# Source gathers in four groups of two, attributes' loads from ScalarE's queue, target rows loaded one pair earlier, in an edge-attention kernel

## Chip, cores and metric

The kernel runs on one core of a Trainium2 chip. The metric is the device time of one execution in microseconds (us). Three executions of the kernel before took 5886.15, 5887.58 and 5853.44 us; the median, 5886.15 us, is the time before.

## What is computed

One layer of graph attention over 12,500 nodes with 128 channels and 400,000 edges, the edges sorted by target. Cut to what matters:

```python
msg_src = h @ w_src + b_src                  # h: layer-normed, rectified nodes
msg_dst = h @ w_dst
message = msg_src[edge_src] + msg_dst[edge_dst]
rad_w   = mlp(edge_attr_32)                  # 32 -> 64 -> 64 -> 128, SiLU
message = message * edge_weight * rad_w
message = message @ w_sep + b_sep            # 8 heads: 16 alpha, 16 value channels each
score   = sum(leaky(alpha) * alpha_dot)      # per edge and head
att     = segment_softmax(score, edge_dst)
out     = segment_sum(value * att, edge_dst) @ w_proj + b_proj
```

The result is added to the node input. All arithmetic is float32, apart from a split of the target rows into three bfloat16 parts.

## The kernel before, in words

The nodes' products come first and are written to two tables in device memory, `t_src` and `t_dst`. The main part, `windows()`, goes over the edges in 400 pairs of two sections. A section has 500 edges in four tiles of 125, so a pair has eight tiles. The sections' edges are sorted by target, so a section touches a window of 64 target rows.

The order of work is written out by hand in `step(k)` (L955). Each engine executes its own instructions in that order; semaphores set by the framework make one engine wait for another. One call of `step(k)` holds work of several pairs, so that they overlap:

- Loads on SyncE's queue (SP), three to six pairs ahead: edge weights (`load_w`, L716), target rows (`load_md`, L720, with two addresses read from `base`, L722), targets (`load_d`, L709, on odd k, for two pairs), edge attributes (`load_e`, L705: 125 x 8 x 32 numbers in runs of 128 bytes), stores of window sums (L926, L929), scores (L841) and maxima (L875).
- Gathers of source rows on GpSimd (POOL): `gather(k, f)` (L739) issues four indirect DMAs (L744), one for each tile of section f, into a tile `gs0` or `gs1` with four buffers. It stands behind `sources(k, f)` (L803), which reads the buffer that the gather refills for the pair four later.
- TensorE (PE), in this order in a step: third layer of the attributes' network of pair k (`mlp3`, L795); transposes of section 1's gathered rows (`sources`, L808) into the PSUM tile `pm1`; `message` (L816), which adds the target rows by a one-hot product; values of the first section of pair c = k - 12 (L908); alpha product of section 0 (`alphas`, L825); first layer of pair k + 2 (L763); values of the second section of c (L908); transposes of section 0 of pair k + 1 (L808, `pm0`); alpha product of section 1 (L825); second layer of pair k + 1 (L778); window sums of c (`sums`, L919); transposes of the attributes of pair k + 3 (`e_T`, L754); on odd k the scores of two pairs (`scores`, L836).
- VectorE (DVE): `rad` (L799) from the third layer and the edge weights, `mT` (L821) from `pm0`, `pm1` and `rad`, `al` (L829) and `pvx` (L910) among others.
- ScalarE (ACT): the SiLUs `sl` (L827), `h1` (L766) and `h2` (L781), the copies `ob` (L923) and `eT` (L756), casts of target rows (`split_md`, L730 and L735) and others. In the loop it issues no DMA.

Most PSUM tiles have one buffer; `V`, `pa`, `misc`, `p3`, `pm0` and `pm1` are each reused in every step. After the last pair the values of the last twelve pairs use `pm0` and `pm1` (L905). The softmax over eight pairs and the combination of windows at the end are not touched by the change.

## Time and profile before

| what | value |
|---|---|
| median of three executions | 5886.15 us |
| profiled execution: time, span | 5892.37 us, 5890.6 us |
| mean granted TensorE clock | 0.892 of full speed |
| busy: TensorE, VectorE, ScalarE, GpSimd | 78%, 53%, 32%, 53% of the span |
| gathers (L744) | 3,200, 970 ns each |
| moved by DMA | 794.76 MB, mean 135 GB/s |
| issues of attributes' loads on SP (L707) | 400 |
| PE waiting for gathered rows (L808) | 1.6 us, once |

The span is the stretch from the first to the last instruction of the profiled execution. Busy times are unions of the instructions of an engine; a busy TensorE is not one at its peak, since the ends of its products are modelled. In rows of waits the columns are: engine and line that waited, what released it, us in total, times, longest. "issue" there means that the profile shows nothing that was waited for, "remote" that the releaser isn't known. In a timeline the columns are: start, length, engine, line, operation, and in brackets the idle time of the engine before it with what ended it. The granted clock of TensorE is 1.00 or 0.50 at any moment; a mean is given for a stretch.

### The profile page before, as it was taken

The page shows a single profiled execution, that of the slowest core. Times are in us where ns is not written, and L with a number is a line of the kernel's source. Part 1 is how long each engine was busy: PE and PEld are TensorE (multiplying, and loading weights), DVE is VectorE, ACT ScalarE, POOL GpSimd, SP SyncE. Part 2 cuts the span into 40 slices and gives each one's busy share as a digit, 9 for nine tenths or more (in the row PEclk, how much of TensorE's full clock was granted, in tenths as well). Part 3 has the DMA queues.
Part 4 walks back from the last instruction along what each step waited for, and adds up shares of the span by engine and source line. Part 5 has one row for each costly group of instructions (what it writes and reads, how often), then busy time and mean ns, then how long its engine had stood idle before and what let it go on. Part 6 is the DMA issues. An engine that isn't in the chain of part 4 may idle for free.

```text
span 5890.6 us, 88077 instructions
## 1 busy us (share of the span) xinstructions
PE 4616.9 (78%) x29692; PEld 2541.0 (43%) x29692; DVE 3100.6 (53%) x6005; ACT 1909.7 (32%) x4595; POOL 3119.2 (53%) x3223
## 2 busy tenths in 40 slices
PE   5688788787877788777877887787887887787874
PEld 3244444444444444444444444444444444444444
DVE  5345555555555555555555554555555555455566
ACT  4233333333333333333333333333333333333331
POOL 1655555555555555555555555555555555555520
PEclk8788988898989999899898998999998989888897
DMA  5565555555555555555565555555555555555533
GB/s 194 156 142 133 136 129 135 139 138 128 143 129 139 144 131 135 132 138 132 137 139 132 140 132 129 128 132 131 137 130 135 127 132 136 127 132 127 132 89 143
DMA packets 901338, 794.76 MB, mean 135 GB/s; under 512 B 530271, under 2 KB 776975, under 8 KB 900747
## 3 DMA queue, kind: packets, MB, share of 16 engines
q1 hardware_dynamic: 796664, 572.15, 36.4%
q0 software_dynamic: 102816, 210.37, 17.9%
q10 hardware_dynamic: 1394, 6.53, 0.3%
q8 instruction: 234, 3.83, 0.3%
q14 instruction: 230, 1.88, 0.1%
HBM read 648.39 MB, written 140.67 MB: 134 GB/s over the span
## 4 chain that ended last, share of the span: by engine, by line
PE 70%; another core or an unknown queue 9%; DVE 8%; issue 7%; ACT 4%; DMA 1%; SPq 1%; POOL 0%; ACTq 0%; POOLq 0%; DVEq 0%
PE V L908 14%; PE pa L825 13%; PE pm L808 8%; PE p L795 8%; PE misc L919 7%; PE pm L816 5%; PE misc L836 4%; PE p L763 4%; PE p L778 4%; PE m L754 3%; DVE mT L821 2%; DVE rad L799 2%; DVE pvx L910 1%; ACT sl L827 1%
## 5 line engine op out<-in xcount | busy, mean ns | idle before, releaser
L744 POOL DMA_INDIRECT gs<-t_src,idx x3200 | 3104.8, 970 | 2537.2 <-PE pm L808 1152.5
L827 ACT ACTIVATE sl<-pa,c_b_a 128x500 f32<-128x500 f32 x800 | 541.9, 677 | 2419.9 <-PE pa L825 1302.9
L825 PE MATMUL pa<-mT,c_w_a 128*128 128x500 f32 x1600 | 933.4, 668 | 451.4 <-DVE mT L821 276.0
L908 PE MATMUL V<-c_w_v,mT 128*125 128x128 f32 x6208 | 987.6, 307 | 198.3 <-DVE pvx L910 171.7
L799 DVE SCALAR_TENSOR_TENSOR rad<-p,c_fc_b,w_b 128x500 f32<-128x500 f32 x800 | 553.2, 733 | 1096.5 <-PE p L795 623.9
L908 PEld LDWEIGHTS V<-c_w_v,mT 128*125 128x125 f32 x6208 | 829.3, 207 | 518.7 <-issue 274.7
L829 DVE SCALAR_TENSOR_TENSOR al<-pa,sl 128x500 f32<-128x500 f32 x800 | 542.3, 678 | 654.3 <-ACT sl L827 396.0
L910 DVE TENSOR_TENSOR pvx<-V,Pem 125x512 f32<-125x512 f32 x776 | 533.2, 687 | 588.7 <-remote 180.6
L821 DVE SCALAR_TENSOR_TENSOR mT<-pm,c_b_src,rad 128x500 f32<-128x500 f32 x800 | 555.1, 733 | 207.4 <-remote 112.2
L919 PE MATMUL misc<-pvx,oh 125*64 125x136 f32 x6400 | 475.7, 292 | 123.2 <-DVE oh L898 75.1
L808 PE MATMUL pm<-ident,gs 125*128 125x125 f32 x3200 | 561.2, 303 | 1.6 <-DMA gs<-t_src,idx 1.6
L808 PEld LDWEIGHTS pm<-ident,gs 125*128 125x128 f32 x3200 | 404.3, 156 | 343.9 <-issue 341.6
L795 PE MATMUL p<-h,w3b 64*128 64x500 f32 x1600 | 495.8, 699 | 34.5 <-ACT h L781 27.1
L919 PEld LDWEIGHTS misc<-pvx,oh 125*64 125x64 f32 x6400 | 372.2, 141 | 290.1 <-issue 183.1
L825 PEld LDWEIGHTS pa<-mT,c_w_a 128*128 128x128 f32 x1600 | 267.7, 210 | 511.0 <-DVE mT L821 310.9
L836 PE MATMUL misc<-al,w_s 128*32 128x500 f32 x1600 | 243.5, 679 | 236.9 <-ACT ob L923 122.9
L816 PE MATMUL pm<-ohT,m 64*128 64x500 bf16 x2400 | 340.6, 392 | 0.0
L763 PE MATMUL p<-eT,w1b 64*128 64x250 f32 x1600 | 309.4, 467 | 1.0 <-ACT eT L756 1.0
L923 ACT COPY ob<-misc 128x136 f32<-128x136 f32 x400 | 109.0, 273 | 619.4 <-PE m L754 308.2
L781 ACT ACTIVATE h<-p,b 128x500 f32<-128x500 f32 x400 | 269.8, 674 | 97.5 <-remote 77.4
L778 PE MATMUL p<-h,w2b 64*64 64x250 f32 x3200 | 278.7, 421 | 9.2 <-ACT h L766 7.7
L766 ACT ACTIVATE h<-p,b 128x500 f32<-128x500 f32 x400 | 272.9, 682 | 27.3 <-remote 14.9
(145 smaller groups left out, 3259.2 us busy)
## 6 DMA issues: line engine op xcount, KB each, us to landing
w_b<-in_edge_weight SPq DMA_DIRECT2D x400, 500.0 KB
d_b<-in_dst SPq DMA_DIRECT2D x400, 250.0 KB
gs<-t_src,idx POOLq DMA_INDIRECT x3200
e_t<-in_edge_attr SPq DMA_DIRECT2D x400, 125.0 KB
sc_d<-Sp SPq DMA_DIRECT2D x200, 250.0 KB
win<-ob SPq DMA_DIRECT2D x400, 68.0 KB
agg<-ob SPq DMA_DIRECT2D x800, 33.5 KB
md<-t_dst SPq DMA_DIRECT2D x800, 32.0 KB
```

Source lines behind the costliest of these rows:

```text
L744: nc.gpsimd.indirect_dma_start(out=gs[:, j, :], out_offset=None, in_=t_src[:, :], in_offset=bass.IndirectOffsetOnAxis(ap=idx[:, t:t + 1], ...
L763: nc.tensor.matmul(p1[:, q, 0:2 * T], w1b[s, :], eTs[k][s, :], start=True, stop=True)
L795: nc.tensor.matmul(p3[:, f, 0:SEC], w3b[s, :], h2s[k][s, :], start=True, stop=True)
L799: nc.vector.scalar_tensor_tensor(rad[:, s], p3[:, f, 0:SEC], b3, w_g[k][:, s], op0=ALU.add, op1=ALU.mult)
L808: nc.tensor.matmul(pms[k, f][:, t * T:(t + 1) * T], gs[:T, t, :], ident[:T, :T], start=(t == 0), stop=False, is_transpose=True, skip_group ...
L816: nc.tensor.matmul(pm[f], m3[k][s, j, :], ohT[k][s, :], start=False, stop=(j == 2), skip_group_check=True)
L821: nc.vector.scalar_tensor_tensor(mTs[k][:, s], pm[f], b_n, rad[:, s], op0=ALU.add, op1=ALU.mult)
L825: nc.tensor.matmul(pa, w_a, mTs[k][:, f * SEC:(f + 1) * SEC], start=True, stop=True)
L827: nc.scalar.activation(sl, pa, AF.Silu, bias=b_a, scale=1.0)
L908: nc.tensor.matmul(V[:, t, :], mTs[c][:, o:o + T], w_v, start=True, stop=True)
L910: nc.vector.tensor_mul(pvx[c][:, f, :, 0:C].rearrange("p t (h k) -> p t h k", h=H), V.rearrange("p t (h k) -> p t h k", h=H), Pem[c // MP] ...
L919: nc.tensor.matmul(acc[f * W:(f + 1) * W, :], ohs[c][:, f * TS + t, :], pvx[c][:, f, t, :], start=(t == 0), stop=(t == TS - 1), skip_group ...
```

## The change

- A gather group is split: `gather(k, f, h)` and `sources(k, f, h)` handle two tiles each, h = 0 or 1, with tiles `gs00`, `gs01`, `gs10`, `gs11` of half the size and four buffers each. The number of gathers, transposes and bytes stays.
- The four groups have new places in `step`. For pair k + 1: section 0's first half where the whole section stood (ahead of the second alpha product), its second half behind that product, section 1's first half behind the window sums and the softmax, ahead of `e_T`. Section 1's second half stays behind `mlp3` in the pair's own step.
- `load_e` is issued on ScalarE's queue and stands behind `alphas(k, 0)`; before it was on SP's, at the beginning of the step.
- `load_md` runs four pairs ahead instead of three, with five buffers instead of four.

```diff
             def load_e(k):
                 e_g[k] = lp.tile([T, 8, RAD], F32, name="e_t", bufs=4)
-                nc.sync.dma_start(out=e_g[k], in_=ea_t[k])
+                nc.scalar.dma_start(out=e_g[k], in_=ea_t[k])
...
-                md[k] = lp.tile([P, C], F32, name="md", bufs=4)
+                md[k] = lp.tile([P, C], F32, name="md", bufs=5)
...
-            def gather(k, f):
-                gs = lp.tile([P, TS, C], F32, name=f"gs{f}", bufs=4)
+            def gather(k, f, h):
+                gs = lp.tile([P, TS // 2, C], F32, name=f"gs{f}{h}", bufs=4)
                 idx, _ = prep[k // 16]
-                for j in range(TS):
-                    t = k % 16 * 8 + f * TS + j
+                for j in range(TS // 2):
+                    t = k % 16 * 8 + f * TS + h * 2 + j
...
-            def sources(k, f):
-
-                gs = gath.pop((k, f))
-                pms[k, f] = pp.tile([C, SEC], F32, name=f"pm{f}")
-                for t in range(TS):
-                    nc.tensor.matmul(pms[k, f][:, t * T:(t + 1) * T], gs[:T, t, :], ident[:T, :T],
+            def sources(k, f, h):
+
+                gs = gath.pop((k, f, h))
+                if h == 0:
+                    pms[k, f] = pp.tile([C, SEC], F32, name=f"pm{f}")
+                for j in range(2):
+                    t = 2 * h + j
+                    nc.tensor.matmul(pms[k, f][:, t * T:(t + 1) * T], gs[:T, j, :], ident[:T, :T],
...
                 if has(k + 3):
                     load_w(k + 3)
-                    load_md(k + 3)
+                if has(k + 4):
+                    load_md(k + 4)
...
-                if has(k + 6) and k >= -4:
-                    load_e(k + 6)
...
                 rad = mlp3(k) if has(k) else None
                 if has(k):
-                    sources(k, 1)
+                    sources(k, 1, 1)
                 if has(k + 4):
-                    gather(k + 4, 1)
+                    gather(k + 4, 1, 1)
...
                     alphas(k, 0)
+                if has(k + 6) and k >= -4:
+                    load_e(k + 6)
...
                 if has(k + 1):
-                    sources(k + 1, 0)
+                    sources(k + 1, 0, 0)
                 if has(k + 5):
-                    gather(k + 5, 0)
+                    gather(k + 5, 0, 0)
                 if has(k):
                     alphas(k, 1)
+                if has(k + 1):
+                    sources(k + 1, 0, 1)
+                if has(k + 5):
+                    gather(k + 5, 0, 1)
...
                     elif r == 3:
                         softmax_T(m - 1)
+                if has(k + 1):
+                    sources(k + 1, 1, 0)
+                if has(k + 5):
+                    gather(k + 5, 1, 0)
                 if has(k + 3):
                     e_T(k + 3)
```

More of the change, by code (lines that the diff above doesn't have):

```diff
@@ L746, in gather @@
                         in_offset=bass.IndirectOffsetOnAxis(ap=idx[:, t:t + 1], axis=0))
-                gath[k, f] = gs
+                gath[k, f, h] = gs
             def e_T(k):
```

## The prediction, made before the result was known

> **What bounds the kernel now.** I read the page first (busy shares, the chain that ended last), then the waits of every engine, then the timeline and the granted clock of a few steps in the middle of the pair loop.
>
> ```profile
> PE 4616.9 (78%) x29692; PEld 2541.0 (43%) x29692; DVE 3100.6 (53%) x6005; ACT 1909.7 (32%) x4595; POOL 3119.2 (53%) x3223
> PE 70%; another core or an unknown queue 9%; DVE 8%; issue 7%; ACT 4%; DMA 1%; SPq 1%; POOL 0%; ACTq 0%; POOLq 0%; DVEq 0%
> ```
>
> TensorE (PE) makes the time, but 30% of the chain is not PE's; the DMA share of the chain is 1%, so no load or gather that arrives late holds the end. The chain in order of time gives the length of a step, from one third-layer product (L795) to the next:
>
> ```profile
> 3003.85 1.04 PE p L795 x4
> 3019.57 1.04 PE p L795 x4
> 3028.85 1.04 PE p L795 x4
> ```
>
> 15.7 us and then 9.3 us. Over pairs 20 to 380 the mean is 13.9 us; the shortest steps take 9.27 us. An odd pair has one product group more (L836, 1.05 us), but odd steps take some 17 us against 10 us for even ones. So some 4 us a pair are lost. Where, the waits of PE tell:
>
> ```profile
> PE pa L825 <- DVE mT L821: 276.0, 164, 5.1
> PE V L908 <- DVE pvx L910: 171.7, 66, 5.4
> PE pa L825 <- issue: 127.6, 57, 22.2
> PE misc L836 <- ACT ob L923: 122.9, 53, 5.7
> PE misc L836 <- issue: 88.5, 78, 2.0
> PE misc L880 <- ACT ob L923: 53.1, 37, 3.9
> ```
>
> PE waits for VectorE and ScalarE, which are busy 53% and 32%. They are late because they learn late that PE is done. The timeline shows it:
>
> ```profile
> 3082.46 0.95 POOL L744 DMA_INDIRECT gs<-t_src,idx  x1 [0.30 <-PE V L908]
> 3083.22 1.10 PE L825 MATMUL pa<-mT,c_w_a 128*128 128x500 f32 x2 [1.25 <-issue]
> 3086.22 0.94 POOL L744 DMA_INDIRECT gs<-t_src,idx  x1 [0.30 <-issue]
> 3089.22 0.69 DVE L910 TENSOR_TENSOR pvx<-V,Pem 125x512 f32<-125x512 f32 x1 [5.41 <-remote]
> 3089.31 1.28 ACT L827 ACT_TABLE_LOAD   x1 [7.11 <-remote]
> 3093.14 1.03 POOL L744 DMA_INDIRECT gs<-t_src,idx  x1 [5.99 <-PE pm L808]
> ```
>
> L825's product ended at 3084.3, and ScalarE, which waits for it, moved at 3089.3. Set against the trace's semaphore updates, this is a rule of the loop: PE's updates come in bursts, and where the last gather on GpSimd (POOL) started over 1.8 us earlier, next to none of them (under 1%) is over 0.3 us late. While POOL issues gathers, 24, 55, 43 and 46% of them are (first to fourth gather of a group), with mean delays over all updates of 0.40, 0.82, 0.60 and 0.46 us. They come free mostly 1.8 to 2.0 us after the start of a group's last gather, when POOL stands. VectorE's and ScalarE's own updates take 11 and 9 ns in the median. I take this as a coupling that the trace shows, without knowing its cause.
>
> POOL's own waits show the same thing at the head of a group:
>
> ```profile
> POOL gs L744 <- PE pm L808: 1152.5, 314, 9.4
> POOL gs L744 <- issue: 763.9, 2491, 1.1
> POOL gs L744 <- PE p L778: 160.1, 117, 1.7
> POOL gs L744 <- PE V L908: 130.6, 109, 1.6
> ```
>
> Inside a group a gather follows 0.31 us behind the one before (763.9 / 2491); a head that only needs an update already due stands 1.2 to 1.4 us (130.6 / 109, 160.1 / 117).
>
> **The change part by part.**
>
> *Gathers in twos.* The count stays at 3,200, of 970 ns each. What changes is that a group has two gathers. Mean delay of an update over four positions: (0.40 + 0.82 + 0.60 + 0.46) / 4 = 0.57 us. Keeping a first and a last: (0.40 + 0.46) / 2 = 0.43 us, 25% less. The PE waits that begin with a late update are the six rows above (839.8 us) and, from the same list, 45.6 (L919, issue) and 17.5 us (L880, issue): 903 us. A quarter is 226 us. Bounds: nothing, because the total time in which POOL issues is the same; and one half (451 us), because the longest block of a group, from 0.8 us after its first gather to 1.8 us after its last one's start, falls from 0.8 to 5.55 (4.75 us) to 0.8 to 3.05 (2.25 us). I take the quarter, which is measured by position.
>
> *The clock.* Mean granted clock is 0.892 and the record has only 1.0 and 0.5, so 0.108 / 0.5 of 5890.6 us, 1272 us, ran at half speed. At the loop's PE share (160 of every 200 us) that costs up to 1272 x 0.5 x 0.8 = 509 us. Windows of 2 us show what leads to it (columns: stretch, length, busy PE, PEld, DVE, ACT, POOL, clock, DMA share, GB/s):
>
> ```profile
> 3006.00:3008.00 2.00, 1.27 (x10) 0.95 (x8) 1.04 (x2) 0.32 (x3) 1.03 (x2) 1.00 0.55 114
> 3008.00:3010.00 2.00, 0.69 (x2) 0.30 (x2) 1.82 (x4) 0.00 (x0) 1.01 (x2) 0.93 0.85 272
> 3010.00:3012.00 2.00, 2.00 (x6) 0.51 (x4) 0.96 (x3) 0.86 (x2) 1.70 (x2) 0.50 0.50 153
> ```
>
> A single gap of 2.04 us (before L825 at 3009.32) was enough; over the loop's 163 drops PE was busy 35% (median) of the 3.4 us before. I let this cost fall with the gaps: a quarter, 127 us. Bounds: 0 and one half (255 us). The Trainium skill (TensorE: Matmul & The Clock Gate, section "HAM oscillation") says that gaps over about 3.4 us of idle PE throttle the clock. By that rule, with every block capped at 2.25 us, all 509 us would come back; the 2.04 us gap above speaks against it, and the measurement decides.
>
> *Two transposes moved ahead of the third layer* (L808, first half of section 1): 0.43 us a group of four in the chain, 0.22 us for two. Now they stand between L795 and L825 and help to cover the way L795, rad (2 x 733 ns, overlapping), mT, L825. In an undisturbed even step L825 starts 3.3 us after L795 with a gap of 0.0 to 0.2 us: PE's own work in between is 1.04 + 0.43 to 0.58 + 0.74 + 1.07 = 3.3 to 3.4 us, VectorE's way the same. So the cover is just gone: 0.22 us stands in front of L795 and L825 comes no sooner (their own needs, the gathers and a free pm1, are met long before). After odd steps the wait before L836 (1.19 us in the mean) hides it; ahead of odd pairs nothing does: 200 x 0.22 = 44 us. Bounds 0 and 88 us.
>
> *Second half of section 0 moved behind L825's second product*: PE's sum is the same, L825 waits there for al, which was ready 0.6 us before in even steps; its 0.22 us comes sooner by no more than that. Nothing, 0 to +40 us.
>
> *Update of L795.* Now 0.15 us late in the mean in even steps, 0.60 us in odd ones (where the group before still runs). With a group triggered behind the sums (L919) I take the middle in even steps: 0.23 x 200 = 46 us; bounds 0 and 0.45 x 200 = 90 us.
>
> *Two more heads a pair on POOL.* Each needs an update of PE: (1.3 - 0.3) x 2 = 2.0 us of POOL a pair. Now POOL needs 8 x 0.97 + 6 x 0.31 + 2 x 1.3 = 12.2 us a pair, then 14.2 us if every head stands, 10.0 us if none does. A POOL that is behind finds its updates there, and the gathers run four pairs ahead, so I take 0; bound +120 us (first rival).
>
> *Attributes' loads from ScalarE.* SP loses 400 issues of 0.46 to 0.51 us and a wait for L754; nothing behind them (the store L931, load_sm) is on the chain (SPq 1%). ScalarE gains them behind sl, ahead of L735 and L766, whose result L778 takes. The load waits for L754 of a step before and for an earlier transfer; both are past when sl has run. In even steps L766 ends at 6.6 us and L778 starts at 8.0 us (means), 1.4 us of cover. So 0; if it were uncovered 400 x 0.46 = 184 us. One store behind such a load took 2.98 us to issue; ScalarE's queue has no second DMA behind it. Bounds -20 and +184 us.
>
> *Rows of targets four pairs ahead*, fifth buffer: the same two address reads and two transfers a pair, at the same place on SP; L730 waited for them 4.2 us in all. 0.
>
> **Sum.** 226 + 127 - 44 - 46 = 263 us. The profiled execution took 5892.4 us (span 5890.6, 1.8 us around it), which is 6.2 us over the median of 5886.15. 5892.4 - 263 = 5629; against the median 5623. I say 5630 us.
>
> **The rivals.**
>
> *POOL becomes the bound (slower).* If every head stands 1.3 us, a pair takes 14.2 us on POOL against 13.9 us now: 0.3 x 400 = 120 us, 6010 us. It decides once PE's own pair falls below 14.2 us while heads still stand. For it: 708 of 800 groups now come with an extra wait instruction for the head, and most heads stand. Against: 94 times two groups ran through without standing between them, so a POOL that is behind catches up.
>
> *The gaps only change place (no change).* POOL issues for as long as before, so as many of PE's updates are caught; the quarter is 0 and with L795's update and the transposes the sum is 0 to 90 us: 5890, at most 5980 us. For it: middle gathers are worst not because they are in the middle, but because of what PE does then.
>
> *A large gain.* Half of the late-update waits and half of the half-clock time go: 451 + 255 - 90 = 616 us, 5270 us. For it: the longest stalls (5 us) need a group of four. Against: only some gaps are that long.
>
> **How the numbers follow.** The forecast has 0.50 (5450 to 5820 us by itself), the large gain 0.09 (5200 to 5450), no change 0.17, of which 0.01 below and 0.04 above 1%, POOL as the bound 0.24 (5945 to 6150). About 1% is what a measurement of this kernel can tell from no change. Faster by over 1% (below 5827): 0.50 + 0.09 + 0.01 = 0.60; same 0.12; slower 0.24 + 0.04 = 0.28. The range 5400 to 6020 us leaves out 0.07 below and 0.12 above.
>
> **What would show it.** Right: PE's idle time before L825 and L908 falls by a quarter, the "remote" waits of L910 and L827 shrink, longest ones from 5 us to about 3, the granted clock rises to about 0.91. Even steps would take 9.5 us at best. Wrong: PE waits for gs (now 1.6 us) would show POOL as the bound; L795's wait for L781 would show ScalarE's issue in the way; unchanged gaps with POOL in twos would show that the coupling is not a matter of a group's length.

## The result and the profile after

The changed kernel took 6163.97 us (median of four executions, 6146.42 to 6174.31), beside 5884.87 us for the kernel before: a ratio of 1.0477, 95% interval 1.0441 to 1.0514. The forecast was 5630 us. The profiled execution of the changed kernel took 6146.42 us (span 6144.6), at a mean granted clock of 0.882.

In two sets of runs below, one of them on a chip that in another set gave 5891 us, the kernel before took about 4600 us, and each ratio is therefore to a kernel before that ran on the same chip in the same set.

Line numbers of the changed kernel are two higher than before from the transposes on (L808 is now L810, L825 is L827, L908 is L910, and so on); L744 and L795 stay. Busy time and the chain that ended last, from the page:

```profile
PE 4741.6 (77%) x29692; PEld 2635.2 (43%) x29692; DVE 3095.0 (50%) x6005; ACT 1952.1 (32%) x4595; POOL 3133.6 (51%) x3223
...
PE 71%; DVE 9%; issue 9%; another core or an unknown queue 7%; ACT 2%; DMA 2%; SPq 0%; POOL 0%; ACTq 0%; POOLq 0%; DVEq 0%
```

TensorE (PE) executes the same 29,692 products; its busy time rose by 125 us at the lower clock. The chain has 9% of issue (7% before) and 2% of DMA (1%): nothing new ends last. From the chain in order of time, the length of three steps (start, length, engine, tile, line):

```profile
3002.94 1.10 PE p L795 x4
...
3012.49 1.04 PE p L795 x4
...
3026.36 1.04 PE p L795 x4
...
3040.09 1.04 PE p L795 x4
```

9.6, 13.9 and 13.7 us. Over pairs 20 to 380 the mean step went from 13.91 to 14.52 us: 0.608 x 400 = 243 us of the 254 us between the spans. Even steps went from 10.57 to 12.14 us, odd ones from 17.26 to 16.90: the loss is in the even steps. PE's waits, the rows that answer to those of before:

```profile
PE pa L827 <- DVE mT L823: 410.6, 148, 28.1
PE pa L827 <- issue: 165.1, 83, 5.1
PE pa L827 <- DVE rad L799: 148.4, 82, 3.2
PE V L910 <- DVE pvx L912: 112.8, 55, 3.9
PE misc L838 <- issue: 85.7, 95, 3.6
PE misc L838 <- ACT ob L925: 72.8, 46, 4.3
...
PE misc L882 <- ACT ob L925: 50.3, 29, 3.7
```

The waits before the alpha product rose (the first row from 276.0 to 410.6; a wait that ends with rad, L799, from 17.1 to 148.4), those before the values fell (171.7 to 112.8), those before the scores fell for L925's copy (122.9 to 72.8), and L882, which waits for the same copy, stayed (53.1 to 50.3). As gaps of PE over 0.3 us between 600 and 5600 us: before the alpha products 369 before, 613 after; before the values 188 and 114; before the scores 219 and 142. VectorE's (DVE's) waits say what is late for the alpha product:

```profile
DVE rad L799 <- PE pm L818: 532.9, 161, 6.4
...
DVE rad L799 <- PE p L795: 340.1, 93, 9.1
DVE rad L799 <- PE V L910: 249.7, 46, 6.5
...
DVE pvx L912 <- remote: 101.6, 39, 4.3
```

rad needs only the third layer (L795). All of PE's products raise one semaphore, and a row names the product that ended last before the update came. Where a later product is named as rad's releaser (L818, L910), the third layer's update had not yet been seen when that product ended. The row with the message (L816 before, L818 now) went from 163.6 to 532.9 us. The values' side gained: pvx's "remote" row fell from 180.6 to 101.6. GpSimd (POOL) waits at more heads, 2775 us in all beside 2537:

```profile
POOL gs L744 <- PE pm L810: 1480.3, 477, 8.6
POOL gs L744 <- issue: 732.5, 2363, 0.7
...
POOL gs L744 <- PE V L910: 112.0, 70, 1.8
```

PE waited for gathered rows (L810) twice, 5.1 us in all: POOL isn't the bound. How the groups lie in time, from the timeline (start, length, engine, line, operation, idle time before it and its releaser):

```profile
3009.47 0.94 POOL L744 DMA_INDIRECT gs<-t_src,idx  x1 [2.60 <-PE pm L810]
...
3012.42 1.11 PE L795 MATMUL p<-h,w3b 64*128 64x500 f32 x4
3013.21 0.94 POOL L744 DMA_INDIRECT gs<-t_src,idx  x1 [0.30 <-issue]
...
3015.21 0.27 ACT L925 COPY ob<-misc 128x136 f32<-128x136 f32 x1 [3.63 <-PE pm L818]
...
3015.38 1.38 DVE L799 SCALAR_TENSOR_TENSOR rad<-p,c_fc_b,w_b 128x500 f32<-128x500 f32 x2 [3.29 <-PE pm L818]
...
3015.51 0.94 POOL L744 DMA_INDIRECT gs<-t_src,idx  x1 [1.36 <-PE pm L818]
...
3017.47 1.11 PE L827 MATMUL pa<-mT,c_w_a 128*128 128x500 f32 x2 [1.77 <-DVE rad L799]
...
3022.10 0.94 POOL L744 DMA_INDIRECT gs<-t_src,idx  x1 [1.90 <-PE pm L810]
...
3026.29 1.11 PE L795 MATMUL p<-h,w3b 64*128 64x500 f32 x4
...
3028.34 0.94 POOL L744 DMA_INDIRECT gs<-t_src,idx  x1 [0.30 <-issue]
...
3030.06 1.38 DVE L799 SCALAR_TENSOR_TENSOR rad<-p,c_fc_b,w_b 128x500 f32<-128x500 f32 x2 [5.73 <-PE V L910]
```

Four gathers start from 3009.47 to 3013.21, 1.25 us apart: both twos of section 0. The sums ended at 3011.91, and their copy (L925) starts only at 3015.21; the third layer ended at 3013.53, and rad starts at 3015.38, 1.85 us later. The next stretch starts at 3015.51 (the two behind the sums), and section 1's other two follow in it without a pause. From 3022.10 to 3028.34 six gathers start in a row, over the end of the step: the third layer ended at 3027.40, rad starts 2.66 us later. An update's lateness is counted here from a product's end to the next recorded update of PE's semaphore; the trace of before has 7,479 records for 8,566 updates, so single values are rough. In the mean over the loop the third layer's update came 0.60 us late in even steps and 1.00 us in odd ones (before 0.15 and 0.68), the sums' 2.16 and 1.31 us (1.16 and 1.23). Two later traces of the changed kernel have 0.55 and 0.61 to 0.62 us for the third layer and 1.73 to 1.78 and 1.13 to 1.14 us for the sums: the rise in even steps is in all three, that in odd ones is not. All of PE's updates together were about 0.6 us late in the mean before, and 0.68, 0.59 and 0.60 us in the three traces of the change: the mean lateness of an update can't explain the loss.

### The profile page after: what moved, and what is told of

It is laid out like the page before. It is cut to its first block, busy times and chain, and to the rows that moved or that the text cites. A ratio compares the mean times of both kernels' runs of the same rounds, so it can differ in the third digit from the quotient of the medians.

```text
span 6144.6 us, 88478 instructions
## 1 busy us (share of the span) xinstructions
PE 4741.6 (77%) x29692; PEld 2635.2 (43%) x29692; DVE 3095.0 (50%) x6005; ACT 1952.1 (32%) x4595; POOL 3133.6 (51%) x3223
## 4 chain that ended last, share of the span: by engine, by line
PE 71%; DVE 9%; issue 9%; another core or an unknown queue 7%; ACT 2%; DMA 2%; SPq 0%; POOL 0%; ACTq 0%; POOLq 0%; DVEq 0%
PE pa L827 14%; PE V L910 14%; PE pm L810 8%; PE p L795 7%; PE misc L921 7%; PE pm L818 7%; PE p L763 5%; PE misc L838 4%; PE p L778 4%; DVE rad L799 4%; DVE mT L823 2%; PE m L754 2%; DVE pvx L912 1%; PE misc L882 0%
## 5 line engine op out<-in xcount | busy, mean ns | idle before, releaser
L744 POOL DMA_INDIRECT gs<-t_src,idx x3200 | 3119.1, 975 | 2775.2 <-PE pm L810 1480.3
L827 PE MATMUL pa<-mT,c_w_a 128*128 128x500 f32 x1600 | 1004.5, 714 | 756.3 <-DVE mT L823 410.6
L799 DVE SCALAR_TENSOR_TENSOR rad<-p,c_fc_b,w_b 128x500 f32<-128x500 f32 x800 | 553.6, 734 | 1471.7 <-PE pm L818 532.9
L910 PE MATMUL V<-c_w_v,mT 128*125 128x128 f32 x6208 | 1040.2, 318 | 126.1 <-DVE pvx L912 112.8
L910 PEld LDWEIGHTS V<-c_w_v,mT 128*125 128x125 f32 x6208 | 876.7, 218 | 464.2 <-issue 273.9
L810 PE MATMUL pm<-ident,gs 125*128 125x125 f32 x3200 | 705.3, 305 | 6.9 <-DMA gs<-t_src,idx 5.1
L810 PEld LDWEIGHTS pm<-ident,gs 125*128 125x128 f32 x3200 | 420.5, 155 | 658.5 <-issue 650.4
L827 PEld LDWEIGHTS pa<-mT,c_w_a 128*128 128x128 f32 x1600 | 288.5, 225 | 839.8 <-DVE mT L823 445.2
L795 PE MATMUL p<-h,w3b 64*128 64x500 f32 x1600 | 483.3, 683 | 7.5 <-ACT h L781 4.9
L925 ACT COPY ob<-misc 128x136 f32<-128x136 f32 x400 | 108.8, 272 | 919.0 <-PE pm L818 294.6
L763 PE MATMUL p<-eT,w1b 64*128 64x250 f32 x1600 | 339.8, 508 | 2.2 <-ACT eT L756 2.2
L818 PE MATMUL pm<-ohT,m 64*128 64x500 bf16 x2400 | 340.8, 392 | 0.0
L763 PEld LDWEIGHTS p<-eT,w1b 64*128 64x128 f32 x1600 | 143.8, 220 | 362.7 <-issue 356.0
L781 ACT ACTIVATE h<-p,b 128x500 f32<-128x500 f32 x400 | 271.5, 679 | 79.6 <-PE p L778 36.0
```

What stands on the lines that cost most here:

```text
L744: nc.gpsimd.indirect_dma_start(out=gs[:, j, :], out_offset=None, in_=t_src[:, :], in_offset=bass.IndirectOffsetOnAxis(ap=idx[:, t:t + 1], ...
L763: nc.tensor.matmul(p1[:, q, 0:2 * T], w1b[s, :], eTs[k][s, :], start=True, stop=True)
L795: nc.tensor.matmul(p3[:, f, 0:SEC], w3b[s, :], h2s[k][s, :], start=True, stop=True)
L799: nc.vector.scalar_tensor_tensor(rad[:, s], p3[:, f, 0:SEC], b3, w_g[k][:, s], op0=ALU.add, op1=ALU.mult)
L810: nc.tensor.matmul(pms[k, f][:, t * T:(t + 1) * T], gs[:T, j, :], ident[:T, :T], start=(t == 0), stop=False, is_transpose=True, skip_group ...
L818: nc.tensor.matmul(pm[f], m3[k][s, j, :], ohT[k][s, :], start=False, stop=(j == 2), skip_group_check=True)
```

## The experiments

All ratios are with 95% intervals. Theories at the start: "place" (the groups' new places put late updates where nothing has slack), against ScalarE's issues, the transposes' order on PE, and the number of heads.

**First set: the parts one by one.** The loads alone:

```diff
-                nc.sync.dma_start(out=e_g[k], in_=ea_t[k])
+                nc.scalar.dma_start(out=e_g[k], in_=ea_t[k])
...
-                md[k] = lp.tile([P, C], F32, name="md", bufs=4)
+                md[k] = lp.tile([P, C], F32, name="md", bufs=5)
...
-                    load_md(k + 3)
+                if has(k + 4):
+                    load_md(k + 4)
...
-                if has(k + 6) and k >= -4:
-                    load_e(k + 6)
...
                     alphas(k, 0)
+                if has(k + 6) and k >= -4:
+                    load_e(k + 6)
...
```

> The kernel before with only the loads changed: attributes' loads issued by ScalarE behind the first alpha product, rows of targets four pairs ahead with five buffers. Gathers in two groups of four as before. Theory 'place' (the loss is that the four groups run together through the end of a step, where updates of the sums and of the third layer have no slack): no difference, 5885 us, within 40. Rival 'ScalarE's issues' (the loads are late or in the way of h1 and sl): all or most of the loss is here, 6100 to 6160 us. The forecast's own steps: 5865 to 5890.

The split alone is the change without those lines:

> The kernel before with only the gathers and transposes split in four groups of two at their new places; all loads as before. Theory 'place': the whole loss, 6130 to 6190 us. Rival 'ScalarE's issues': 5885 or less. The forecast's own steps (groups of two are shorter, fewer updates late): 5630 us, which would need the loads to cost 500.

Section 0's split alone, and section 1's alone (the other section stays one group of four):

```diff
-                    sources(k + 1, 0)
+                    sources(k + 1, 0, 0)
...
-                    gather(k + 5, 0)
+                    gather(k + 5, 0, 0)
...
                     alphas(k, 1)
+                if has(k + 1):
+                    sources(k + 1, 0, 1)
+                if has(k + 5):
+                    gather(k + 5, 0, 1)
```

> The kernel before with only section 0 split: first half ahead of the second alpha product, second half behind it; section 1 whole, four gathers behind the third layer, as before. Theory 'place': the second half starts later and runs nearer to the sums, but nothing is triggered behind the sums: a part of the loss, 5900 to 6020 us. Rival 'transposes on TensorE' (the loss is that two transposes left the gap between third layer and alpha): none of it here, 5885. A rule of 'number of heads' (every further group costs the same): half, 6020.

```diff
-                    sources(k, 1)
+                    sources(k, 1, 1)
...
-                    gather(k + 4, 1)
+                    gather(k + 4, 1, 1)
...
                         softmax_T(m - 1)
+                if has(k + 1):
+                    sources(k + 1, 1, 0)
+                if has(k + 5):
+                    gather(k + 5, 1, 0)
```

> The kernel before with only section 1 split: first half behind the sums, second half behind the third layer; section 0 whole, four gathers ahead of the second alpha product, as before. Theory 'place': most of the loss, 6030 to 6160 us, since the group behind the sums runs over the third layer's update. Rival 'transposes on TensorE': as much, 6100 to 6160 (told apart by the order alone in a later run). 'Number of heads': half, 6020.

Measured: in this set the kernel before took 4585.87 us. Loads alone 4472.18 us, 0.9747 [0.9721, 0.9773]; split alone 4568.95, 0.9966 [0.9951, 0.9981]; section 0 alone 4591.66, 1.0014 [0.9994, 1.0033]; section 1 alone 4565.92, 0.9956 [0.994, 0.9971]. None of the expectations for the split came true, because the thing that they were about was missing: with the loads alone PE's updates were 0.03 us late in the mean, 2% of them over 0.3 us (0.6 us and 46% in the trace of before). The starts of the engines show the same without the records: ScalarE, where it waited for an alpha product, started over 0.3 us after the product's end in 27% of 749 cases before and in under 1% of 741 here, while PE, where it waited for mT, started 53 ns after VectorE's end in the median in both traces. The gathers were no different, as the page's row shows (busy, mean ns of one, idle before and what ended most of it). Here the loads alone in this set:

```profile
L744 POOL DMA_INDIRECT gs<-t_src,idx x3200 | 3086.7, 965 | 1149.4 <-issue 808.2
```

and the same kernel in a later set, where the kernel before took 5891.2 us:

```profile
L744 POOL DMA_INDIRECT gs<-t_src,idx x3200 | 3100.9, 969 | 2547.2 <-PE pm L808 1136.6
```

965 and 969 ns a gather; only POOL's waits for PE differ. The timelines of the two, first this set:

```profile
3005.81 0.94 POOL L744 DMA_INDIRECT gs<-t_src,idx  x1 [0.30 <-issue]
...
3009.06 1.11 PE L795 MATMUL p<-h,w3b 64*128 64x500 f32 x4
...
3010.22 1.38 DVE L799 SCALAR_TENSOR_TENSOR rad<-p,c_fc_b,w_b 128x500 f32<-128x500 f32 x2 [3.48 <-PE p L795]
...
3011.02 0.94 POOL L744 DMA_INDIRECT gs<-t_src,idx  x1 [0.52 <-PE pm L808]
...
3012.39 1.03 PE L825 MATMUL pa<-mT,c_w_a 128*128 128x500 f32 x2
...
3013.46 0.68 ACT L827 ACTIVATE sl<-pa,c_b_a 128x500 f32<-128x500 f32 x1 [3.14 <-PE pa L825]
3013.51 1.00 POOL L744 DMA_INDIRECT gs<-t_src,idx  x1 [0.30 <-issue]
```

POOL issues nearly without a pause, yet rad starts 0.05 us after the third layer's end (3010.17) and sl 0.04 us after the alpha product's (3013.42). Then the other:

```profile
3009.17 1.15 POOL L744 DMA_INDIRECT gs<-t_src,idx  x1 [0.30 <-issue]
...
3014.38 0.94 POOL L744 DMA_INDIRECT gs<-t_src,idx  x1 [0.30 <-issue]
...
3015.63 0.95 POOL L744 DMA_INDIRECT gs<-t_src,idx  x1 [0.30 <-issue]
...
3015.90 1.78 PE L825 MATMUL pa<-mT,c_w_a 128*128 128x500 f32 x2 [3.36 <-issue]
...
3019.41 0.69 DVE L910 TENSOR_TENSOR pvx<-V,Pem 125x512 f32<-125x512 f32 x1 [2.92 <-PE p L763]
```

The alpha product waits 3.36 us, behind the seventh gather of a row that began at 3007.92. So where updates are prompt, gathers hold none back, however long a stretch is. What follows: the split's loss can't be explained by work or by POOL's time alone; it comes only with the late updates.

**Second set: the change again, blocks of eight, no gathers.**

> The changed kernel itself once more, beside the kernel before on the same chip. In the first four experiments the kernel before took 4586 us, not 5885, and next to none of TensorE's updates came late. If that belongs to the chip and not to the kernels, the sign of the change goes with it: where updates come late (before 5885), 6160 us again; where they are prompt (before 4586), the sum of loads (-114 us) and split (-17 us), 4455 us, a gain. If the loss belongs to the change itself, some 4.8% over the kernel before in either place.

```diff
                     gather(k + 4, 1)
+                    gather(k + 4, 0)
...
-                if has(k + 5):
-                    gather(k + 5, 0)
```

> The kernel before, with section 0's gathers of pair k + 4 put on GpSimd right behind section 1's of the same pair (no new wait: their buffers came free a step before). All eight gathers of a pair run in one block from the third layer on; TensorE's order is untouched. Where updates come late: theory 'place' (only sums and third layer have no slack) 5600 to 5900 us, as the block ends before the next third layer in long steps; theory 'length' (the forecast's: a longer block is worse wherever it stands) over 6000. Where updates are prompt: 4586 us, within 50.

```diff
-                if has(k + 4):
-                    gather(k + 4, 1)
...
                     gather(k + 5, 0)
+                if has(k + 4):
+                    gather(k + 4, 1)
```

> The kernel before, with section 1's gathers put on GpSimd behind section 0's of the step, ahead of the second alpha product: one block of eight from there, over the sums and into the next third layer and alpha; TensorE's order is untouched. Where updates come late: theory 'place' as slow as the changed kernel or slower, 6100 to 6500 us, and at least 200 over the block behind the third layer; theory 'length' the same time as that block. Where updates are prompt: 4586 us, within 50.

```diff
             def gather(k, f):
+                if k >= 4:
+                    gath[k, f] = old[k % 4, f]
+                    return
...
-                gath[k, f] = gs
+                gath[k, f] = old[k, f] = gs
```

> The kernel before without its gathers from the fifth pair on: the transposes read the first four pairs' rows again, so 3,168 of 3,200 gathers are left out and the sums are not the reference's. If GpSimd's issuing is what holds TensorE's updates, then where they come late the time falls from 5885 to about what it is where they are prompt, 4450 to 4600 us, with a clock of 0.97 or more; if something else on that chip holds them, it stays over 5500. Where updates are prompt: 4400 to 4586 us (loads and stores have more of the DMA engines).

Measured: before 5877.41 us. The change again 6184.34, 1.0488 [1.041, 1.0566]. The block behind the third layer 6877.0, 1.1688 [1.1606, 1.1771]; the block ahead of the second alpha product 6692.31, 1.135 [1.1271, 1.143]. Without gathers 4466.27, 0.7587 [0.7535, 0.764].

Without gathers no update of PE in the loop was over 0.04 us late, and PE is busy 93% of the span (the page's line of busy times):

```profile
PE 4148.2 (93%) x29692; PEld 2313.7 (52%) x29692; DVE 3074.0 (69%) x6005; ACT 1908.4 (43%) x4595; POOL 44.8 (1%) x55
```

So the gathers are what holds the updates; leaving them out takes 1411 of 5877 us. Whether it is GpSimd's issuing or the transfers that it starts, this run can't tell, since it leaves out both. And "place" fell as I had put it: it gave 5600 to 5900 us for the block behind the third layer. "Length" gave both blocks the same time, and they are 185 us apart, with intervals that don't meet. Behind the third layer the block left its update prompt, as planned (0.02 us late in even steps, 0.09 in odd ones), and this was the slowest kernel of all. The waits have moved to the hops that the block now covers:

```profile
PE p L795 <- ACT h L781: 618.5, 181, 5.1
PE misc L836 <- ACT ob L923: 468.5, 144, 4.5
PE misc L919 <- DVE oh L898: 256.0, 176, 9.2
```

The third layer waits for h2 (L781; 27.1 us in the trace of before, 618.5 here) and the scores for the copy of the sums. Behind a finished alpha product ScalarE idled 1004 us (175 before). What a place decides is which wait it is; eight in a row cost 815 and 1000 us in two different places. Length as such isn't separated from place by this, since a block of eight also lies over hops that two fours leave free.

**Third set: which part, where updates come late.**

> The changed kernel a third time, so that the following three have it beside them. On a chip where the kernel before takes about 5880 us: 6160 to 6190. On one where it takes about 4586: loads (-114) and split (-17) add up, 4455 us; if the two do not add, between 4455 and 4570.

> The kernel before with the loads' change alone, again. Where the kernel before takes about 5880 us: theory 'gathers' (all of the loss is from the split and its places) 5880 us or a little less, at most 60 either way; rival 'ScalarE's issues' 6100 or more. Where it takes 4586: 4472 again.

> The kernel before with the split alone, again. Where the kernel before takes about 5880 us: theory 'gathers' 6130 to 6190 us; rival 'ScalarE's issues' 5880 or less. Where it takes 4586: 4569 again.

PE's order alone (gathers in fours, triggered as before; the halves read the whole section's tile):

```diff
-                    sources(k, 1)
+                    sources(k, 1, 1)
...
                         softmax_T(m - 1)
+                if has(k + 1):
+                    sources(k + 1, 1, 0)
```

> The kernel before with only two transposes moved: section 1's first two go from behind the third layer to behind the sums, as in the change; the gathers stay in fours, triggered as before. Where the kernel before takes about 5880 us: theory 'gathers' 5880 to 5930 us (the forecast's own step has +44); rival 'order' (the loss is the cover that left the way from third layer to alpha) 6050 to 6160. Where it takes 4586: 4540 to 4630.

Measured: before 5891.2 us. The change 6192.61, 1.0474 [1.0384, 1.0563]; loads alone 5877.16, 0.9947 [0.9911, 0.9983]; split alone 6112.8 (just under the 6130 to 6190 expected), 1.0345 [1.0247, 1.0444]; order alone 5770.69, 0.9746 [0.9655, 0.9837]. The loss is the split's; ScalarE's issues cost nothing, and whether the loads add something on top of the split stays open, since the intervals of split and change overlap. The order alone was expected to cost 0 to 50 us and gained 1.6 to 3.5% by the interval (three executions of 5735.54 to 5775.05 us; a fourth took 18860.02 us and is not in the ratio). Its waits of PE show where (L837 is the scores):

```profile
PE pa L826 <- DVE mT L822: 294.0, 167, 27.8
...
PE misc L837 <- issue: 65.7, 79, 1.9
...
PE misc L837 <- ACT ob L924: 47.7, 39, 5.6
```

The two transposes now stand in the wait ahead of the scores, which fell from 219 to 102 us of gaps; the alpha product's gaps stayed (369 and 372), those before the sums rose from 77 to 143 us, and odd steps went from 17.26 to 16.07 us while even ones went from 10.57 to 11.18 us.

**Fourth set: which group, and twos against fours.** The first two kernels are those of the first set.

> The kernel before with only section 0 split: twos ahead of and behind the second alpha product; section 1 whole behind the third layer, as before. Where the kernel before takes about 5880 us: theory 'closing up' (a group that is triggered while the one before it still runs, or just has run, makes one longer stretch, and the group behind the sums joins the third layer's) 5880 to 5960 us, as the two twos make about the old four; theory 'twos cost by themselves' (more heads, more stretches) 6000 or more. Where it takes 4586: 4592 again.

> The kernel before with only section 1 split: two behind the sums, two behind the third layer; section 0 whole ahead of the second alpha product, as before. It holds the moved transposes that alone gained 120 us. Where the kernel before takes about 5880 us: theory 'closing up' 6030 to 6130 us, most of the split's loss, since the four ahead of the alpha, the two behind the sums and the two behind the third layer follow one another; theory 'twos cost by themselves' about 5900, as the moved transposes pay for half. Where it takes 4586: 4566 again.

The whole order of the change on PE, with gathers in fours:

```diff
-                if has(k + 5):
-                    gather(k + 5, 0)
                 if has(k):
                     alphas(k, 1)
+                if has(k + 1):
+                    sources(k + 1, 0, 1)
+                if has(k + 5):
+                    gather(k + 5, 0)
...
+                if has(k + 1):
+                    sources(k + 1, 1, 0)
```

> The kernel before with TensorE's whole order of the change (all four moved halves of the transposes), and the gathers in two groups of four: section 1's behind the third layer's transposes, section 0's behind its second half, one alpha product later than before. The split alone differs from it by the groups alone. Where the kernel before takes about 5880 us: theory 'closing up' 5750 to 5900 us, at least 200 under the split alone; if TensorE's order makes the loss, 6050 or more. Where it takes 4586: 4540 to 4600.

The order alone and the loads together:

> The two parts that did not lose: section 1's first two transposes behind the sums, gathers in fours as before, and the loads' change. Where the kernel before takes about 5880 us: 5770 less up to 15 from the loads, 5740 to 5790 us. Where it takes 4586: 4472 or a little less, 4430 to 4490.

Measured: before 5868.13 us. Section 0 alone 5939.58, 1.0123 [1.0049, 1.0196]; section 1 alone 6545.51, 1.1146 [1.1059, 1.1234]; order with fours 5857.45, 0.9985 [0.9954, 1.0016]; order and loads 5773.89, 0.9848 [0.9772, 0.9923]. Section 0 alone, the order with fours, and order and loads lie where "closing up" or the parts' sum had put them; section 1 alone is some 400 us over the 6030 to 6130 us of "closing up": right in sign, far off in size.

Section 1's split alone loses over twice what the whole change does. It differs from the order alone of the third set by its gathers and their tiles only, so triggering two of section 1's four behind the sums takes the ratio from 0.9746 to 1.1146. Its timeline (gs0None is the tile of section 0's four, L745 the gather, L824 is mT, L828 the alpha product):

```profile
3005.08 1.43 POOL L745 DMA_INDIRECT gs0None<-t_src,idx  x1 [2.81 <-PE pm L811]
...
3009.32 0.94 POOL L745 DMA_INDIRECT gs0None<-t_src,idx  x1 [0.30 <-issue]
...
3010.56 0.94 POOL L745 DMA_INDIRECT gs<-t_src,idx  x1 [0.30 <-PE pm L819]
...
3013.99 1.39 DVE L824 SCALAR_TENSOR_TENSOR mT<-pm,c_b_src,rad 128x500 f32<-128x500 f32 x2 [2.99 <-remote]
3014.31 0.94 POOL L745 DMA_INDIRECT gs<-t_src,idx  x1 [0.30 <-issue]
...
3014.78 2.03 PE L828 MATMUL pa<-mT,c_w_a 128*128 128x500 f32 x2 [3.69 <-issue]
```

Section 0's four start from 3005.08; the two behind the sums and the two behind the third layer follow with no pause, the head at 3010.56 0.30 us behind the gather before it. Eight in a row, from the second alpha product over the sums, the third layer and the message to the next alpha product, which waits 3.69 us and then runs at half clock (2.03 us): the block of eight of the second set, made by three groups that close up. With section 0 split as well the split as a whole is at 1.0345. Its section 0 is still a four: 99% of the second twos follow the first without a pause (98% after the change). But POOL stands ahead of the two behind the sums in 41% of the steps, beside 12% for section 1 alone; that this makes the difference is argued, not shown. And with PE's order the same, fours instead of twos are at 0.9985.

To put a number on closing up, I count a stretch as gathers that start at most 1.7 us after one another (inside a group it is 1.25 us) and take the share of gathers in stretches of six or more, between 600 us and 500 us before the end:

| kernel | share in stretches of six or more | updates held, us | idle behind a finished product, us | us |
|---|---|---|---|---|
| order and loads | 3% | 1850 | 1346 | 5774 |
| order with fours | 6% | 1949 | 1666 | 5857 |
| section 0 alone | 9% | 1908 | 1393 | 5940 |
| order alone | 12% | 1857 | 1385 | 5771 |
| loads alone | 19% | 1908 | 1370 | 5877 |
| before | 24% | 1966 | 1326 | 5885 |
| the change (three traces) | 29%, 43%, 44% | 1947, 1831, 1847 | 1795, 1706, 1734 | 6164 to 6193 |
| split alone | 36% | 1815 | 1722 | 6113 |
| section 1 alone | 59% | 1846 | 1758 | 6546 |
| block ahead of the alpha product | 82% | 2045 | 1968 | 6692 |
| block behind the third layer | 99% | 2139 | 1984 | 6877 |

The next two columns are for the same stretch of time. The third is the time in which a finished product of PE had no update yet. The fourth is the time in which VectorE or ScalarE stood idle although the product that its next instruction reads had ended (what goes over 0.1 us of such a hop, eight kinds of hop; 1 us for the loads alone in the first set). The updates were held for nearly as long in all eleven kernels. What differs is on which hops, and so who waits: in the three traces of the change more behind the third layer (rad: 448 to 489 us, before 190) and behind the sums (their copy: 468 to 575, before 320), less behind the values (pvx: 183 to 216, before 338) and the alpha product (sl: 95 to 114, before 175). The fourth column goes with the time only roughly: the order with fours has 1666 us and is no slower than before.

From a quarter on, share and time broadly rise together; below it other things decide. The share of long stretches is an order among eleven kernels, not a law: with 2.0 us as the bound the classes are the same (19 to 38%, 48 to 61%, 81%, 100%), with 2.5 us they are no longer told apart, and a stretch also gets longer because a trigger comes while POOL is still behind. The causal part is the built blocks and section 1 alone, where only the gathers were moved. The version that beats both kernels is the order alone, with or without the loads.

**Fifth set: a single four against two separate twos, with half of the gathers.**

```diff
+                for h in range(2):
+                    if h and k >= 4:
+                        halves.append(old[k % 4, f])
+                        continue
```

> The kernel before with half of its gathers: from the fifth pair on only the first two of each section are issued, so a pair has two groups of two, in the old places; the other transposes read the first four pairs' rows again, and the sums are not the reference's. Where the kernel before takes about 5880 us, and 4466 without gathers: its eight gathers cost 1410 us. The forecast's rule by position: half of that times 0.43 / 0.57, 530, so 5000 us. If only the number of gathers counts: 5170, as for the single four. Theory 'length of a stretch': under 4900, and at least 200 under the single four. Where the kernel before takes 4586: 4470 to 4590.

```diff
+                if k >= 4 and f == 0:
+                    gath[k, f] = old[k % 4]
+                    return
```

> The kernel before with half of its gathers: from the fifth pair on section 1's four are issued in the old place behind the third layer, section 0's are left out (its transposes read the first four pairs' rows again, and the sums are not the reference's). Where the kernel before takes about 5880 us, and 4466 without gathers: half the loss, 5170 us, by the forecast's rule and if only the number counts; theory 'length of a stretch' 5050 to 5300, and at least 200 over the two twos. Where the kernel before takes 4586: 4470 to 4590.

Both kernels leave out half of the gathers. Measured: 4459.62 us, 0.967 [0.9647, 0.9693], and 4459.01, 0.9668 [0.9645, 0.9691], beside 4610.79 for the kernel before. Updates were prompt in this set (0.1% of those of the twos were over 0.3 us late), so the question was not put: whether two separate twos hold fewer updates than one four stays open. Half of the gathers left out gained 3.3% here all the same, so gathers cost time by another way too; which, no run here separates.

## Why the prediction was wrong

*Gathers in twos: -226 us.* This is the step that failed. It kept the mean delay of a first and of a last gather, and so took it that the groups stay apart and that a saved delay counts the same on any hop. "One half, because the longest block falls from 4.75 to 2.25 us" rests on the same. The groups don't stay apart: section 0's two twos run as one four in 98 to 99% of the steps, and each of section 1's twos follows the gather before it without a pause in 50 to 59% (traces of the change and of the split). POOL needs 10 us of a step of 14 for its gathers, so a new trigger behind the sums falls into the stretch before it or runs into the third layer's group. And the updates were held for 1831 to 1947 us, as long as before (1966), but VectorE and ScalarE stood behind finished products for 1706 to 1795 us instead of 1326. That the gathers' new triggers make the loss, and not PE's order, is shown by the split beside the order with fours (1.0345 and 0.9985) and by section 1 alone beside the order alone (1.1146 and 0.9746); why a hold falls on one hop and not on another is not shown.

Of its signs the values' side came (their waits fell, and pvx's "remote" row); the alpha product's side did not (PE's gaps before it rose, and ScalarE's "remote" row stayed, 215.3 and 216.3 us). Nearly so did the sign that it had against itself, unchanged gaps with POOL in twos: PE's gaps over 0.3 us between 600 and 5600 us are 985 us before and 1036 us after. The quarter was not well measured either. Counted from a product's end to the next recorded update, the trace of before has 0.71, 1.09, 0.73 and 0.72 us by position, not 0.40, 0.82, 0.60 and 0.46; a first and a last are then 12% under the mean of four, not 25%. The prediction had a number against the step in its own text: 94 double groups in the trace of before, used there as a point against POOL being the bound.

*The clock: -127 us.* Wrong in sign, since it was tied to the first step. Time at half clock went from 1272 to 1447 us; at PE's share of 0.79 that is 175 x 0.5 x 0.79 = +69 us. The half-clock time is 1052 us for the order alone and 2543 us for the block behind the third layer, so it goes with the gaps, as assumed (905 and 1259 us of gaps over 0.3 us in the same stretch, 985 before). The Trainium skill (TensorE: Matmul & The Clock Gate, section "HAM oscillation") puts the limit at idle gaps of about 3.4 us; in the changed kernel's loop 50 of 205 drops of the clock had a gap over 3.4 us in the 8 us before, and 56 had none over 2 us, so the trace again doesn't bear the limit out.

*Two transposes moved ahead: +44 us.* The price of a short step was right: the first percentile of all steps rose from 9.27 to 9.48 us, and 0.22 was the price. In the mean, even steps of the order alone rose by 0.61 us, and odd ones fell by 1.19 us. The odd step had the wrong sign: I let the wait before the scores hide the transposes there and credited nothing for taking them off the third layer's side. Alone, the order gained 2.5%, with 117 us fewer gaps before the scores and 66 us more before the sums. Whether the cover itself does it, or section 1's trigger that comes two transposes sooner, was not separated.

*Second half of section 0: 0 to +40 us.* Alone, with its gathers, +72 us by the ratio (interval +29 to +115). Together with section 1's split it is the other way round: 1.1146 without it, 1.0345 with it.

*Update of the third layer: +46 us (0 to 90).* The place was right, the size was at its upper bound: 0.40 to 0.45 us more in even steps in the three traces are 80 to 90 us, if each counts in full. The 0.32 us more in odd steps (64 us) is in one trace of three. The sums' update, which the prediction did not count, came 0.57 to 1.0 us later in even steps.

*Heads on POOL: 0.* Right: PE waited for gathered rows 5.1 us. The rival that ended on the slower side was right in sign for a reason that the trace refutes; the rival "gaps only change place" had the mechanism, as many updates held as before and a quarter of 0, but with up to 90 us of loss it priced only the third layer's update and the transposes, and not the sums' copy, nor that VectorE and ScalarE would stand some 400 us longer behind finished products.

*Loads on ScalarE and target rows: 0.* Right where updates come late: 0.5% less by the ratio, 10 to 52 us by its interval, just outside the -20 us that I had as a bound. The two loads' changes were run only together.

In sum, 353 us of gain did not come. By ratios of separate sets, the split's twos cost 1.0345 / 0.9985 = 3.6% against fours with PE's whole order the same, and 1.0345 / 0.9746 = 6% against the order alone, which is the best that fours alone did.

## What to carry to other kernels

Before cutting a queue's work into smaller pieces, lay the pieces' triggers and durations on one step's timeline, and see which of them run together and which engines' waits they then cover, above all across the end of the step. Where an engine is busy for most of a step, a later trigger may not spread its work but join it to the next. Whether a shorter group costs less when it does stay alone is not shown here. A mean delay is a poor price: in this kernel the delays stayed and only moved to hops that are waited for. And try the parts of a change alone: here a part costed as a small loss was the largest gain where updates came late.

## What the runs showed of the hardware

- Where GpSimd issues indirect DMAs, TensorE's semaphore updates can come late by up to 7.2 us (loop of the kernel before), and without such DMAs they don't (at most 0.04 us). With them left out, the kernel takes 4466 us instead of 5877; not all of that need be late updates, as half of the gathers left out gained 151 us where updates were prompt. VectorE's updates were not held: where PE waited for mT, it started 53 ns after mT's end in the median, with and without the lateness.
- This is in some sets of runs and not in others, for the same kernel: 5891 us in one set and 4611 us in another on the same chip. The loads' run has 969 and 965 ns a gather in two such sets. What makes the difference stays open. Every time here has a recorded span and clock, and the traces with late updates hold fewer records of semaphore updates (50,797 beside 120,031 for the loads' run); whether recording itself has a part in the lateness, no run here shows.
- Where updates are prompt, POOL issues with next to no pause (stretches of over a hundred gathers in the loads' run), PE is busy 91 to 93% at a clock of 0.97 to 0.98, and what is worth something changes: the loads on ScalarE gain 2.5% there and 0.5% where updates are late, while section 1's split is 0.4% faster there and 11% slower here. The whole change was not run in such a set; its two parts point to a gain.
